# Last layer's attention: fp32 products of 8 rows become bf16 products of 24 rows in three passes

## The chip, the cores and the metric

The kernel runs on one core of a Trainium2 chip. The metric is the device time of one execution in microseconds. All durations below come from one profiled execution and its trace.

## The reference

The reference is a small network of four layers. Each layer normalises x, runs a token mixer s and a feed-forward g on the normalised x, and adds s times silu(g) to x. There are 4 batches of 1024 tokens with 128 channels. Only the last layer is touched here. Its mixer is causal attention with relative positions: 16 heads of 8 channels.

```python
qx, kx, vx = (split_head(x @ W.T) for W in (Wq, Wk, Wv))       # [b, 16, n, 8]
ex = rel_embed[ns].reshape(n, NH, HD).transpose(1, 0, 2)       # [16, n, 8]
srel = srel_skew(jnp.einsum('bhnd,hmd->bhnm', qx, ex))         # pad one column left, reshape, cut
qk = (jnp.einsum('bhnd,bhmd->bhnm', qx, kx) + srel) * inv_dim
atten = jax.nn.softmax(qk - mask, axis=-1)
out = jnp.einsum('bhnm,bhmd->bhnd', atten, vx).transpose(0, 2, 1, 3).reshape(b, n, d)
return out @ Wp.T + bp
```

Here n is 1024 and `ns` counts from -768 to 255, while the table `rel_embed` has 256 rows. The kernel therefore computes the relative term for a band near the diagonal from differences to the table's first row, and further keys get the plain product of q and k. Two einsums, q times k and q times the embeddings, contract over the 8 channels of a head; these two are what the change rewrites.

## The kernel before

Layers 0 to 2 run one after another over all batches and fill the first two thirds of the time. The last layer works batch by batch (`b`), in groups of four heads (`i` = 0 to 3, so 16 groups in all), and within a group over eight tiles of 128 queries (`t`, in the order 7, 0, 6, 1, 5, 2, 4, 3). A batch, group and tile together are a unit.

`prepare3` builds the weights once: transposes of Wq, Wk, Wv and Wp, and the embedding table `emb`. The four heads of a group sit on partitions 0, 32, 64 and 96, eight rows each, so that TensorE can work on four row groups side by side. POOL spreads the table into a zeroed `pad` (L1650), TensorE transposes it, and the first row is subtracted (L1657, L1658).

`begin3` prepares one batch: it loads x, normalises it (`layernorm`: batch-norm instructions on DVE, L136 and L137, square root and scaling on ACT, L138 and L143), transposes it, multiplies by Wq and Wk (L1832), copies the products on ACT (L1833) and stores q and k in DRAM (L1834). For batches 1 to 3 it is a generator that is advanced one step per unit beside the previous batch. `project3` loads q and k of one group back into SBUF, eight rows per head (L1882).

`relative3` multiplies two blocks of q with the table for two heads (L1911). ACT copies the product to a tile `r` (L1913), and SP stores it in a DRAM tile `flat` (L1916, L1917). `shear3` reads `flat` back on a slant into `rel` (L1932 to L1938) and POOL masks it (L1942). The loads for a unit are issued three units ahead.

`scores3` is the core. For each unit and each stretch of up to 512 keys it takes the single PSUM tile `sc`, does four score matmuls (L1975), one per head, and then compares on DVE, head by head: L1983 for keys beyond the band and L1990 for those with a relative term. Both scale, write `neg` and keep the running minimum `low`. After the last stretch ACT takes the exponential (L1997). There are 192 such score tiles. DVE then transposes the weights in blocks of 32 (L1734), one or two score tiles later, and `weigh3` multiplies them with the values (L2011). `finish3` and `end3` normalise, project and store.

`sc` has one buffer (four banks of PSUM), `tr` has three and `o` one. The pool `temp` has three buffers, shared by x, xn, the tiles of q, k and v in `begin3`, the tiles `h` and `up` of the feed-forward and all tiles `r`. The loop in `layer3` sets the rough order by advancing the generators; a compile-time scheduler then orders the instructions of each engine by its own estimates. Every engine, SP's DMA queue included, runs its instructions in that order.

Of the kernel before, what the change touches and what calls it, by code (L numbers as in the profile page):

```python
# [19 lines left out]
P = 128  # L20
NB = 4
T = 1024
# [1592 lines left out]

def spread(a):

    return a.rearrange("p (i j r) -> p i j r", j=4, r=32)[:, :, :, 0:8]


def heads_of(a):
    return a.rearrange("p (i j d) -> p i j d", j=4, d=8)


def prepare3(k, w, W, ps):
    nc = k.nc
    new = lambda name, shape: w.tile(shape, F32, tag=name, name=name)
    for name in ("Wq", "Wk", "Wv"):
        W[name + "T"] = new(name + "T", [P, D])
        k.transpose_tiles(ps, "tr", [W[name]], W[name + "T"])  # L1630

    W["WpB"] = new("WpB", [P, 4, 4, D])
    with k.tc.tile_pool(name="wide3", bufs=1) as rp:
        wide = rp.tile([P, 4, 4, 4, 8], F32, tag="wide", name="wide")
        for a in range(4):
            nc.gpsimd.tensor_copy(wide[:, :, :, a, :], W["Wp"].rearrange("p (i j d) -> p i j d", j=4, d=8))
        for i in range(4):
            pt = ps.tile([P, P], F32, tag="tr", name="pt")
            nc.tensor.transpose(pt, wide[:, i].rearrange("p j a d -> p (j a d)"), k.ident)
            for a in range(4):  # L1640
                nc.vector.tensor_scalar(W["WpB"][:, i, a, :], pt, k.c("of_a")[:, a : a + 1], None, op0=ALU.mult)
    W["bpw"] = new("bpw", [P, D])
    nc.gpsimd.tensor_copy(W["bpw"], W["bp"])
    W["emb"] = new("emb", [P, 4, 256])
    with k.tc.tile_pool(name="pad3", bufs=1) as rp:
        pad = rp.tile([P, 2, 512], F32, tag="pad", name="pad")
        nc.vector.memset(pad, 0.0)
        for c in range(2):
            for i in range(4):
                nc.gpsimd.tensor_copy(spread(pad[:, c, :])[:, i], heads_of(W["rel"][:, c, :])[:, i])  # L1650
        for i in range(4):
            k.transpose_tiles(ps, "tr", [pad[:, c, i * P : (i + 1) * P] for c in (0, 1)], W["emb"][:, i, :])

        e0 = rp.tile([P, 4], F32, tag="e0", name="e0")
        nc.vector.tensor_copy(e0, W["emb"][:, :, 0])
        for i in range(4):
            nc.vector.tensor_scalar(W["emb"][:, i, :], W["emb"][:, i, :], e0[:, i : i + 1], None, op0=ALU.subtract)  # L1657
        nc.vector.tensor_scalar(W["emb"][:, :, 0], e0, -1.0, None, op0=ALU.mult)  # L1658
        for name in ("gate", "up", "down"):
            f = rp.tile([P, 3, D], F32, tag="f" + name, name="f" + name)  # L1660
            nc.vector.tensor_scalar(f, W[name], 1.0 / 127.0, None, op0=ALU.mult)
            W[name + "T"] = new(name + "T", [P, 3, D])
            k.transpose_tiles(ps, "tr", [f[:, c, :] for c in range(3)], W[name + "T"].rearrange("p c d -> p (c d)"))
# [146 lines left out]
def begin3(k, W, p1, p2, temp, ps, dram, x3, b, eps5, seq):  # L1810

    nc = k.nc
    x = load_x3(nc, temp, x3, b)
    xn = temp.tile([P, 2 * 4, D], F32, tag="temp", name="xn")
    k.layernorm(p2, x.rearrange("p h a d -> p (h a) d"), xn, eps5)
    yield
    seq["xnT"] = xnT = p1.tile([P, T], F32, tag="xnT", name="xnT")
    for half in range(2):
        pt = ps.tile([P, 4, P], F32, tag="tr", name="pt")
        for a in range(4):  # L1820
            nc.tensor.transpose(pt[:, a, :], xn[:, 4 * half + a, :], k.ident)
        dst = xnT[:, half * 512 : (half + 1) * 512].rearrange("p (t a i) -> p a t i", t=4, a=4)
        nc.scalar.copy(dst, pt.rearrange("p a (t i) -> p a t i", i=32))
        yield

    seq["qk"] = dram.tile([2, P, T], F32, tag="qk", name="qk")
    for n, name in enumerate(("WqT", "WkT")):
        qk = temp.tile([P, T], F32, tag="temp", name="qk")
        for half in range(2):
            tok = slice(half * 512, (half + 1) * 512)  # L1830
            pp = ps.tile([P, 512], F32, tag="tr", name="pp")
            nc.tensor.matmul(pp, W[name], xnT[:, tok], start=True, stop=True)  # L1832
            nc.scalar.copy(qk[:, tok], pp)  # L1833
        nc.sync.dma_start(out=seq["qk"][n], in_=qk)  # L1834
        yield
    v = temp.tile([P, NT, D], F32, tag="temp", name="v")
    for half in range(2):
        pv = ps.tile([P, 4, D], F32, tag="tr", name="pv")
        for t in range(4):
            at = (4 * half + t) * P  # L1840
            nc.tensor.matmul(pv[:, t, :], xnT[:, at : at + P], W["WvT"], start=True, stop=True)
        nc.scalar.copy(v[:, 4 * half : 4 * half + 4], pv)
    seq["vd"] = vd = dram.tile([T, D], F32, tag="vd", name="vd")
    nc.sync.dma_start(out=vd.rearrange("(t p) d -> p t d", p=P), in_=v)
# [27 lines left out]

def project3(k, p2, seq, i, group):

    nc = k.nc
    q = p2.tile([P, 1 + T], F32, tag="q", name="q")
    kk = p2.tile([P, T], F32, tag="k", name="k")
    nc.gpsimd.memset(q[:, 0:1], 0.0)
    group.update({"q": q, "k": kk, "sums": p2.tile([P, 4, NT], F32, tag="sums", name="sums")})
    for n, dst in ((0, q[:, 1:]), (1, kk)):  # L1880
        for j in range(4):
            nc.sync.dma_start(out=dst[32 * j : 32 * j + 8], in_=seq["qk"][n, 32 * i + 8 * j : 32 * i + 8 * j + 8])  # L1882
        yield


def values3(k, p1, seq, vb, i):
# [12 lines left out]
def relative3(k, W, temp, ps, flat, q, i, pair, jp):  # L1899

    nc = k.nc
    r = temp.tile([P, 2, 2, 256], F32, tag="temp", name="r")
    js = (2 * jp, 2 * jp + 1)
    pr = [ps.tile([P, 2, 256], F32, tag="tr", name="pr") for _ in js]
    for m in range(2):
        for j, to in zip(js, pr):
            at, t = slice(32 * j, 32 * j + 8), 2 * pair + m  # L1910
            nc.tensor.matmul(to[:, m, :], q[at, t * P : (t + 1) * P], W["emb"][at, i, :], start=True, stop=True)  # L1911
    for n, to in enumerate(pr):
        nc.scalar.copy(r[:, n], to)  # L1913
    rows = flat.rearrange("m j p u -> p j m u")
    for m in range(2):
        nc.sync.dma_start(out=rows[:, 2 * jp : 2 * jp + 2, m, 0:256], in_=r[:, :, m])  # L1916
        nc.sync.dma_start(out=rows[:, 2 * jp : 2 * jp + 2, m, 256:384], in_=r[:, :, m, 0:P])  # L1917
# [37 lines left out]
def scores3(k, p1, p2, ps, group, rel, t):  # L1955
# [5 lines left out]
    nc = k.nc  # L1961
    q, kk = group["q"], group["k"]
    n = (t + 1) * P
    at = lambda j: slice(32 * j, 32 * j + 8)
    size = "b" if t > 3 else "s"
    S = [(p2 if t > 3 else p1).tile([P, T if t > 3 else 512], F32, tag=f"S{size}{j}", name="neg") for j in range(4)]
    group["S", t] = S
# [3 lines left out]
    for first in range(0, n, 512):  # L1971
        last = min(first + 512, n)
        sc = ps.tile([P, 4, 512], F32, tag="sc", name="score")
        for j in range(4):
            nc.tensor.matmul(  # L1975
                sc[:, j, 0 : last - first], q[at(j), 1 + t * P : 1 + n], kk[at(j), first:last], start=True, stop=True
            )
        yield "products"
        for j in range(4):

            neg, m = S[j], low[j]
            if first < plain:
                nc.vector.tensor_scalar(  # L1983
                    neg[:, 0:plain], sc[:, j, 0:plain], -INV3, None, op0=ALU.mult, op1=ALU.min, accum_out=m[:, 0:1]
                )
                least[j] = m[:, 0:1]
            begin = max(first, plain)
            slot = min(t, 4) - t + begin // P
            here = m[:, 1:2] if first == 0 else m[:, 2:3]
            nc.vector.tensor_tensor_reduce(  # L1990
                out=neg[:, begin:last], in0=sc[:, j, begin - first : last - first],
                in1=rel[:, j, slot : slot + (last - begin) // P, :].rearrange("p s c -> p (s c)"),
                scale=-INV3, scalar=least[j], op0=ALU.add, op1=ALU.min, accum_out=here,
            )
# [144 lines left out]
```

## Time and profile before

| What | Value |
|---|---|
| median of 3 runs | 3289.05 us (3281.75 to 3289.76) |
| profiled execution, its own time | 3290.69 us |
| its span, first to last instruction | 3288.7 us |
| PE matmul busy | 2325.6 us (71%) |
| PE weight load busy | 1329.6 us (40%) |
| DVE busy | 2357.9 us (72%) |
| ACT busy | 1487.6 us (45%) |
| POOL busy | 1203.9 us (37%) |
| mean granted TensorE clock | 0.732 of full |
| last layer's score matmuls L1975 | 1536 records, 292.7 us busy |
| last layer's table matmuls L1911 | 1024 records, 240.8 us busy |
| comparisons L1990 | 768 instructions |
| weights times values L2011 | 10240 records, 242.2 us busy |
| DMA through SP's queue | 296.03 MB |

A row with a line number stands for all instructions of that line. "Busy" is the time in which at least one of them runs. One fp32 matmul of the program shows as two matmul records and two weight loads. "Idle before, releaser" is the time that an engine stood still before those instructions, and the instruction that ended it. The pages' rows of digits cut the span into 40 slices and give the busy share of each in tenths; PEclk is the granted clock in tenths.

### The profile page before, as it was taken

The page shows a single profiled execution, that of the slowest core. Times are in us where ns is not written, and L with a number is a line of the kernel's source. Part 1 is how long each engine was busy: PE and PEld are TensorE (multiplying, and loading weights), DVE is VectorE, ACT ScalarE, POOL GpSimd, SP SyncE. Part 2 cuts the span into 40 slices and gives each one's busy share as a digit, 9 for nine tenths or more (in the row PEclk, how much of TensorE's full clock was granted, in tenths as well). Part 3 has the DMA queues.
Part 4 walks back from the last instruction along what each step waited for, and adds up shares of the span by engine and source line. Part 5 has one row for each costly group of instructions (what it writes and reads, how often), then busy time and mean ns, then how long its engine had stood idle before and what let it go on. Part 6 is the DMA issues. An engine that isn't in the chain of part 4 may idle for free. (4 is left out here: it accounts for less than half of the span.)

```text
span 3288.7 us, 50603 instructions
## 1 busy us (share of the span) xinstructions
PE 2325.6 (71%) x18321; PEld 1329.6 (40%) x18321; DVE 2357.9 (72%) x5534; ACT 1487.6 (45%) x3248; POOL 1203.9 (37%) x1104
## 2 busy tenths in 40 slices
PE   5787776777776767966243772557888888888885
PEld 2555555222332323641001322344544555545553
DVE  5555545978888876566899878436778778777786
ACT  3555453433333334345132551125665665655663
POOL 3344434144434343224586323342322322322322
PEclk9888888688778878976555665565767766756776
DMA  3000000100000001210422445337676767766772
GB/s 86 5 1 1 1 1 11 23 0 0 1 0 0 0 0 58 97 64 21 116 80 79 106 102 118 106 95 229 172 213 201 199 204 204 200 205 193 198 227 72
DMA packets 396446, 303.46 MB, mean 92 GB/s; under 512 B 96272, under 2 KB 380812, under 8 KB 390564
## 3 DMA queue, kind: packets, MB, share of 16 engines
q1 hardware_dynamic: 395044, 296.03, 32.0%
q10 hardware_dynamic: 1152, 4.19, 0.4%
q8 instruction: 144, 2.36, 0.3%
q14 instruction: 106, 0.87, 0.1%
HBM read 160.63 MB, written 138.94 MB: 91 GB/s over the span
## 5 line engine op out<-in xcount | busy, mean ns | idle before, releaser
L1997 ACT ACTIVATE neg<-neg,low 128x640 f32<-128x640 f32 (+7 forms) x512 | 390.0, 763 | 163.4 <-DVE low L1990 163.2
L1942 POOL TENSOR_SCALAR_AFFINE_SELECT rel<-rel 128x512 f32<-128x512 f32 x288 | 179.2, 634 | 584.5 <-DMA rel<-flat 420.5
L1734 DVE STREAM_TRANSPOSE wT<-neg 128x640 f32<-128x640 f32 (+7 forms) x512 | 362.4, 754 | 7.4 <-ACT neg L1997 6.3
L1975 PE MATMUL score<-k,q 8*128 8x512 f32 (+3 forms) x1536 | 292.7, 737 | 94.0 <-DVE low L1990 93.6
L1990 DVE CUSTOM_DVE_ANT_0 neg<-score,rel,low 128x128 f32<-128x128 f32 (+3 forms) x448 | 217.5, 517 | 158.7 <-PE score L1975 111.2
L1911 PE MATMUL pr<-emb,q 8*128 8x256 f32 x1024 | 240.8, 556 | 42.2 <-ACT r L1913 28.4
L2011 PE MATMUL po<-wT,vb 128*32 128x64 f32 (+1 forms) x10240 | 242.2, 258 | 35.2 <-issue 19.7
L2011 PEld LDWEIGHTS po<-wT,vb 128*32 128x32 f32 x10240 | 207.2, 140 | 144.7 <-issue 79.5
L1913 ACT COPY r<-pr 128x512 f32<-128x512 f32 x256 | 138.4, 581 | 143.5 <-PE pr L1911 94.3
L1911 PEld LDWEIGHTS pr<-emb,q 8*128 8x128 f32 x1024 | 150.4, 262 | 121.6 <-ACT r L1913 65.1
L1990 DVE CUSTOM_DVE_ANT_0 neg<-score,rel 128x512 f32<-128x512 f32 (+3 forms) x320 | 149.4, 521 | 26.5 <-PE score L1975 9.3
L1975 PEld LDWEIGHTS score<-k,q 8*128 8x128 f32 x1536 | 103.5, 249 | 156.6 <-DVE low L1990 126.9
L214 PE MATMUL pt<-ident,three 128*24 128x128 bf16 x64 | 9.3, 299 | 215.7 <-DVE three L211 211.3
L835 PE MATMUL pg<-xnT,w 128*128 128x512 f32 x256 | 148.2, 662 | 6.7 <-DVE h L839 3.1
L788 POOL TENSOR_TENSOR prod<-rest,kv 128x2048 f32<-128x2048 f32 x32 | 145.2, 4574 | 18.4 <-ACT rest L778 18.4
L837 PE MATMUL pu<-xin,w 128*128 128x512 f32 x256 | 141.2, 635 | 13.7 <-DVE h L839 7.7
L826 PE MATMUL po<-h,w 128*128 128x512 f32 x256 | 131.4, 635 | 26.9 <-DVE h L839 26.9
L838 ACT ACTIVATE h<-pg 128x512 f32<-128x512 f32 x128 | 75.9, 595 | 156.8 <-PE pg L835 153.3
L1983 DVE TENSOR_SCALAR_CACHE_REDUCE neg<-score 128x384 f32<-128x384 f32 (+2 forms) x192 | 79.9, 416 | 69.4 <-PE score L1975 69.4
L1452 PE MATMUL read<-kt,const_sb 128*128 128x128 f32 x256 | 51.3, 378 | 97.8 <-POOL kt L1447 97.8
L1050 PE MATMUL ph<-xin,upT 128*128 128x512 bf16 (+1 forms) x128 | 70.9, 586 | 64.7 <-DVE xin L1044 64.4
L431 PE MATMUL px<-hT,xbcT 128*128 128x512 f32 x256 | 115.8, 597 | 0.0
(621 smaller groups left out, 5788.7 us busy)
## 6 DMA issues: line engine op xcount, KB each, us to landing
flat<-r SPq DMA_DIRECT2D x256, 256.0 KB
rel<-flat SPq DMA_DIRECT2D x112, 512.0 KB
flat<-r SPq DMA_DIRECT2D x256, 128.0 KB
rel<-flat SPq DMA_DIRECT2D x96, 256.0 KB
kt<-kd SPq DMA_DIRECT2D x16, 512.0 KB
qt<-qd SPq DMA_DIRECT2D x16, 512.0 KB
kdc<-kdd SPq DMA_DIRECT2D x16, 512.0 KB
ktc<-ktd SPq DMA_DIRECT2D x16, 512.0 KB
```

The lines of the kernel that those rows point to most:

```text
L788: nc.gpsimd.tensor_tensor(prod, attn.rearrange("p (t h g) -> p t h g", t=4, g=16)[:, t].unsqueeze(2).to_broadcast(each), kv[:, t, 1, :].re ...
L826: nc.tensor.matmul(po, W["w2"][:, e, c, :], h[:, c, :], start=(e == 0 and c == 0), stop=(e == 7 and c == 1))
L835: nc.tensor.matmul(pg, W["w1"][:, e, c * P : (c + 1) * P], xnT, start=True, stop=True)
L837: nc.tensor.matmul(pu, W["w3"][:, e, c * P : (c + 1) * P], xin, start=True, stop=True)
L1734: nc.vector.transpose(weights[at, pair][j][:, t % 2, 0 : (t + 1) * P], S[j][:, 0 : (t + 1) * P])
L1911: nc.tensor.matmul(to[:, m, :], q[at, t * P : (t + 1) * P], W["emb"][at, i, :], start=True, stop=True)
L1913: nc.scalar.copy(r[:, n], to)
L1942: nc.gpsimd.affine_select(out=rel[:, :, slot(back), :], in_=rel[:, :, slot(0), :], compare_op=op, fill=fill, base=0, pattern=[[0, 4], [-si ...
L1975: nc.tensor.matmul(sc[:, j, 0 : last - first], q[at(j), 1 + t * P : 1 + n], kk[at(j), first:last], start=True, stop=True)
L1990: nc.vector.tensor_tensor_reduce(out=neg[:, begin:last], in0=sc[:, j, begin - first : last - first], in1=rel[:, j, slot : slot + (last - b ...
L1997: nc.scalar.activation(neg[:, 0:n], neg[:, 0:n], AF.Exp, bias=here, scale=-1.0, accum_out=group["sums"][:, j, t : t + 1])
L2011: nc.tensor.matmul(o[32 * j : 32 * j + 32, 2 * pair + m.start : 2 * pair + 2, :], vb[:, kb, j].rearrange("p a d -> p (a d)"), weights[j][: ...
```

## The change

q, k and the embeddings are each written as a sum of three bf16 numbers: the value rounded to bf16, the remainder rounded, and the remainder of that. On the contraction axis q has 24 rows per head, three thirds for each of 8 channels. The other operand holds one of its own thirds per pass, repeated three times over those rows, and three passes accumulate in PSUM, so that all nine products of thirds are summed.

- `prepare3` repeats each channel three times in the padded table and splits the transposed fp32 table into three bf16 tables with ACT copies and DVE subtractions.
- `begin3` splits each half of q and k with an ACT copy, a DVE subtraction, an ACT copy and a POOL subtraction, in two tiles of `temp` per half. It stores q once and k three times, and yields after each half.
- `project3` loads 24 rows per head: q of 2 bytes a token, k of three times 2 bytes.
- `relative3` and `scores3` make three bf16 matmuls per product instead of one fp32 matmul, with the thirds in the outer loop and the heads in the inner one.

```diff
 def spread(a):
-    return a.rearrange("p (i j r) -> p i j r", j=4, r=32)[:, :, :, 0:8]
+    return a.rearrange("p (i j r) -> p i j r", j=4, r=32)[:, :, :, 0:24].rearrange("p i j (d a) -> p i j d a", a=3)
...
-    W["emb"] = new("emb", [P, 4, 256])
+    W["emb"] = w.tile([P, 3, 4, 256], BF16, tag="emb", name="emb")
...
-                nc.gpsimd.tensor_copy(spread(pad[:, c, :])[:, i], heads_of(W["rel"][:, c, :])[:, i])
+                for a in range(3):
+                    nc.gpsimd.tensor_copy(spread(pad[:, c, :])[:, i, :, :, a], heads_of(W["rel"][:, c, :])[:, i])
+        emb = rp.tile([P, 4, 256], F32, tag="emb32", name="emb")
...
+        for third in range(3):
+            nc.scalar.copy(W["emb"][:, third], emb)
+            if third < 2:
+                nc.vector.tensor_tensor(emb, emb, W["emb"][:, third], ALU.subtract)
...
-    seq["qk"] = dram.tile([2, P, T], F32, tag="qk", name="qk")
-    for n, name in enumerate(("WqT", "WkT")):
-        qk = temp.tile([P, T], F32, tag="temp", name="qk")
+    seq["q"] = dram.tile([P, 3, T], BF16, tag="qd", name="qd")
+    seq["k"] = dram.tile([P, 3, 3, T], BF16, tag="kd", name="kd")
+    for name in ("WqT", "WkT"):
         for half in range(2):
             tok = slice(half * 512, (half + 1) * 512)
             pp = ps.tile([P, 512], F32, tag="tr", name="pp")
             nc.tensor.matmul(pp, W[name], xnT[:, tok], start=True, stop=True)
-            nc.scalar.copy(qk[:, tok], pp)
-        nc.sync.dma_start(out=seq["qk"][n], in_=qk)
-        yield
+            three = temp.tile([P, 3, 512], BF16, tag="temp", name="three")
+            rest = temp.tile([P, 512], F32, tag="temp", name="rest")
+            nc.scalar.copy(three[:, 0], pp)
+            nc.vector.tensor_tensor(rest, pp, three[:, 0], ALU.subtract)
+            nc.scalar.copy(three[:, 1], rest)
+            nc.gpsimd.tensor_tensor(three[:, 2], rest, three[:, 1], ALU.subtract)
+            if name == "WqT":
+                nc.sync.dma_start(out=seq["q"][:, :, tok], in_=three)
+            else:
+                for a in range(3):
+                    nc.sync.dma_start(out=seq["k"][:, a, :, tok], in_=three)
+            yield
...
-    q = p2.tile([P, 1 + T], F32, tag="q", name="q")
-    kk = p2.tile([P, T], F32, tag="k", name="k")
-    nc.gpsimd.memset(q[:, 0:1], 0.0)
+    q = p2.tile([P, 2 + T], BF16, tag="q", name="q")
+    kk = p2.tile([P, 3, T], BF16, tag="k", name="k")
+    nc.gpsimd.memset(q[:, 0:2], 0.0)
...
-            nc.sync.dma_start(out=dst[32 * j : 32 * j + 8], in_=seq["qk"][n, 32 * i + 8 * j : 32 * i + 8 * j + 8])
+        nc.sync.dma_start(out=q[32 * j : 32 * j + 24, 2:], in_=seq["q"][head].rearrange("d a t -> (d a) t"))
...
+        nc.sync.dma_start(out=kk[32 * j : 32 * j + 24], in_=seq["k"][head].rearrange("d a b t -> (d a) b t"))
...
-            at, t = slice(32 * j, 32 * j + 8), 2 * pair + m
-            nc.tensor.matmul(to[:, m, :], q[at, t * P : (t + 1) * P], W["emb"][at, i, :], start=True, stop=True)
+        first = 1 + (2 * pair + m) * P
+        for third in range(3):
+            for j, to in zip(js, pr):
+                at = slice(32 * j, 32 * j + 24)
+                nc.tensor.matmul(
+                    to[:, m, :], q[at, first : first + P], W["emb"][at, third, i, :], start=(third == 0), stop=(third == 2)
+                )
...
-        for j in range(4):
-            nc.tensor.matmul(
-                sc[:, j, 0 : last - first], q[at(j), 1 + t * P : 1 + n], kk[at(j), first:last], start=True, stop=True
-            )
+        for third in range(3):
+            for j in range(4):
+                nc.tensor.matmul(
+                    sc[:, j, 0 : last - first], q[at(j), 2 + t * P : 2 + n], kk[at(j), third, first:last],
+                    start=(third == 0), stop=(third == 2),
+                )
```

More of the change, by code (lines that the diff above doesn't have):

```diff
@@ L1649, in prepare3 @@
             for i in range(4):
-                nc.gpsimd.tensor_copy(spread(pad[:, c, :])[:, i], heads_of(W["rel"][:, c, :])[:, i])
+                for a in range(3):
+                    nc.gpsimd.tensor_copy(spread(pad[:, c, :])[:, i, :, :, a], heads_of(W["rel"][:, c, :])[:, i])
+        emb = rp.tile([P, 4, 256], F32, tag="emb32", name="emb")
         for i in range(4):
-            k.transpose_tiles(ps, "tr", [pad[:, c, i * P : (i + 1) * P] for c in (0, 1)], W["emb"][:, i, :])
+            k.transpose_tiles(ps, "tr", [pad[:, c, i * P : (i + 1) * P] for c in (0, 1)], emb[:, i, :])
         e0 = rp.tile([P, 4], F32, tag="e0", name="e0")
-        nc.vector.tensor_copy(e0, W["emb"][:, :, 0])
+        nc.vector.tensor_copy(e0, emb[:, :, 0])
         for i in range(4):
-            nc.vector.tensor_scalar(W["emb"][:, i, :], W["emb"][:, i, :], e0[:, i : i + 1], None, op0=ALU.subtract)
-        nc.vector.tensor_scalar(W["emb"][:, :, 0], e0, -1.0, None, op0=ALU.mult)
+            nc.vector.tensor_scalar(emb[:, i, :], emb[:, i, :], e0[:, i : i + 1], None, op0=ALU.subtract)
+        nc.vector.tensor_scalar(emb[:, :, 0], e0, -1.0, None, op0=ALU.mult)
+        for third in range(3):
+            nc.scalar.copy(W["emb"][:, third], emb)
+            if third < 2:
+                nc.vector.tensor_tensor(emb, emb, W["emb"][:, third], ALU.subtract)
         for name in ("gate", "up", "down"):
@@ L1875, in project3 @@
     nc = k.nc
-    q = p2.tile([P, 1 + T], F32, tag="q", name="q")
-    kk = p2.tile([P, T], F32, tag="k", name="k")
-    nc.gpsimd.memset(q[:, 0:1], 0.0)
+    q = p2.tile([P, 2 + T], BF16, tag="q", name="q")
+    kk = p2.tile([P, 3, T], BF16, tag="k", name="k")
+    nc.gpsimd.memset(q[:, 0:2], 0.0)
     group.update({"q": q, "k": kk, "sums": p2.tile([P, 4, NT], F32, tag="sums", name="sums")})
-    for n, dst in ((0, q[:, 1:]), (1, kk)):
-        for j in range(4):
-            nc.sync.dma_start(out=dst[32 * j : 32 * j + 8], in_=seq["qk"][n, 32 * i + 8 * j : 32 * i + 8 * j + 8])
-        yield
+    for j in range(4):
+        head = slice(32 * i + 8 * j, 32 * i + 8 * j + 8)
+        nc.sync.dma_start(out=q[32 * j : 32 * j + 24, 2:], in_=seq["q"][head].rearrange("d a t -> (d a) t"))
+    yield
+    for j in range(4):
+        head = slice(32 * i + 8 * j, 32 * i + 8 * j + 8)
+        nc.sync.dma_start(out=kk[32 * j : 32 * j + 24], in_=seq["k"][head].rearrange("d a b t -> (d a) b t"))
+    yield
 def values3(k, p1, seq, vb, i):
@@ L1908, in relative3 @@
     for m in range(2):
-        for j, to in zip(js, pr):
-            at, t = slice(32 * j, 32 * j + 8), 2 * pair + m
-            nc.tensor.matmul(to[:, m, :], q[at, t * P : (t + 1) * P], W["emb"][at, i, :], start=True, stop=True)
+        first = 1 + (2 * pair + m) * P
[5 more added lines that the diff above has]
+                )
     for n, to in enumerate(pr):
@@ L1963, in scores3 @@
     n = (t + 1) * P
-    at = lambda j: slice(32 * j, 32 * j + 8)
+    at = lambda j: slice(32 * j, 32 * j + 24)
     size = "b" if t > 3 else "s"
@@ L1973, in scores3 @@
         sc = ps.tile([P, 4, 512], F32, tag="sc", name="score")
-        for j in range(4):
-            nc.tensor.matmul(
-                sc[:, j, 0 : last - first], q[at(j), 1 + t * P : 1 + n], kk[at(j), first:last], start=True, stop=True
-            )
+        for third in range(3):
+            for j in range(4):
+                nc.tensor.matmul(
+                    sc[:, j, 0 : last - first], q[at(j), 2 + t * P : 2 + n], kk[at(j), third, first:last],
+                    start=(third == 0), stop=(third == 2),
+                )
         yield "products"
```

## The prediction

> **What bounds the kernel now.** I read four views: the page for the stages, the table by stretches of time for the last layer, the waits inside it, and the timeline for single tiles. Only the last layer is touched: it runs from about 2185 us to the end, its score stream from 2216.57 us (first L1975) to 3265 us.
>
> ```profile
> span 3288.7 us, 50603 instructions
> PE   5787776777776767966243772557888888888885
> DVE  5555545978888876566899878436778778777786
> PEclk9888888688778878976555665565767766756776
> ```
>
> The right half of each row is the last layer: neither PE nor DVE is full, and TensorE's granted clock is about two thirds. The stretches (span, PE, PE load, DVE, ACT, POOL busy, clock, DMA share, GB/s) say the same:
>
> ```profile
> 1900.00:2000.00 100.00, 65.04 (x203) 28.72 (x202) 74.91 (x194) 51.80 (x108) 22.80 (x16) 0.67 0.49 108
> 2200.00:2400.00 200.00, 160.53 (x1985) 104.15 (x1987) 126.66 (x407) 116.04 (x260) 51.19 (x75) 0.65 0.72 206
> 2600.00:2800.00 200.00, 169.22 (x2810) 104.84 (x2809) 159.04 (x507) 119.67 (x284) 51.98 (x73) 0.67 0.71 208
> ```
>
> Two engines at 75 to 85% suggest alternation. The waits of that window (engine, line, releaser: us, times, longest) show it:
>
> ```profile
> POOL rel L1942 <- DMA rel<-flat: 420.5, 80, 16.0
> PEld score L1975 <- DVE low L1990: 126.9, 99, 11.0
> DVE neg L1990 <- PE score L1975: 120.5, 63, 6.8
> DVE neg L1983 <- PE score L1975: 69.4, 15, 25.2
> ```
>
> There is one score tile in PSUM: PE waits until DVE has compared all four heads, then DVE waits for the next scores. Going through the 192 score tiles record by record, in 102 the first comparison starts within 0.22 us of the last score matmul; DVE is idle 228 us there. Score matmuls fill 188 us of those intervals, and in 77 us PE is still busy with something else (weights times values 23, feed-forward 27, table products L1911 11). In the other 90 tiles DVE is still transposing, and a shorter score gives nothing. POOL's 420 us on loads is no bound: DVE waits for POOL's result 17.7 us in all.
>
> **The change: cheaper matmuls.** The granted clock has two values, 0.5 and 1. The timeline has both for the eight records of one tile (start, duration):
>
> ```profile
> 2639.66 1.18 PE L1975 MATMUL score<-k,q 8*128 8x512 f32 x8
> 2645.36 2.07 PE L1911 MATMUL pr<-emb,q 8*128 8x256 f32 x8 [0.92 <-ACT r L1913]
> 2651.36 1.24 PE L1975 MATMUL score<-k,q 8*128 8x256 f32 x8 [0.66 <-DVE low L1990]
> 2654.73 2.09 PE L1975 MATMUL score<-k,q 8*128 8x512 f32 x8 [0.94 <-DVE low L1990]
> ```
>
> At half clock 256 more columns cost 0.85 us, 3.32 ns each: four passes of 0.83 ns. Each fp32 product is two records of two passes, the four heads side by side. At full clock (1.14 for 512, 0.71 for 256) it is 1.7 ns. For bf16 at 24 rows the trace has a near row, the routing product of the expert layers:
>
> ```profile
> L222 PEld LDWEIGHTS <-pick x128: 90/98/110, 623.9 to 1947.8; 24*128 24x128 bf16 x128
> L222 PE MATMUL pb<-thirds,pick x128: 371/580/629, 623.9 to 1947.8; 24*128 24x512 bf16 x128
> ```
>
> One bf16 pass of 512 columns, alone, is 0.60 us at half and 0.37 at full clock. Three are 0.60+2x0.425=1.45 against 2.09, and 0.37+2x0.225=0.82 against 1.14. For 256 columns: 0.82 against 1.24, and 0.48 against 0.71. The table product of two heads (12 records instead of 8) goes from about 2.07 to 1.6 at half clock, 1.13 to 0.85 at full. Clipping each score saving by DVE's idle time, with the clock each tile had, leaves 37 us of the 102 tiles.
>
> The built program's order changes too: the scheduler weighs the new matmuls by its own costs. So I summed all 192 steps: a step is the comparison of four heads, then the later of (transposes behind it) and (next score plus whatever PE work between the two scores overruns the comparison). Prices are the rows above; weights times values 46 matmuls in 2.58 us cold and 1.53 warm; 64% of the time at half clock (0.68 mean). Old order and prices: 1098 us against 1045 measured, 5% too much. Old order, new prices: 1032, so **-66**. New order, new prices: 1084, **-14**. The order gives 52 back: in groups 4, 8 and 12, 158 weights-times-values matmuls (45 ns each, 7.1 us) and some 38 table matmuls (4 us) stand between the two score tiles of t=5, where there were 82 and 1. Comparing takes 3.5 us there, so the next score is some 7 us late; what moved up had been hidden later on. I take -14, with -45 (the order costs a third) and +10 as ends.
>
> **The clock.** The last layer's PE is 82 to 86% busy at 0.65 to 0.73; the stretch 1900 to 2000 is 65% busy and has 0.67, so by these rows the clock does not follow the load, and nothing is added. The Trainium skill ("TensorE: Matmul & The Clock Gate", "What's actually happening") speaks against the change: half speed is the default and some 3.4 us of activity releases it, so PE work cut by a sixth may spend more time cold. With 72% instead of 64% at half clock the sum is 1103, 20 us more. Nearer to the row, I take +4; end +20.
>
> **Start of the layer.** Nothing covers it. The padding is filled by 24 POOL copies instead of 8, 0.204 us each (L1650): +3.3. Then three ACT copies (1.14 us for 128x1024, L1997) and two DVE subtractions (about 1.2 from 0.69 for 128x512, L1582) alternate, and in the new order the batch-norm aggregate of the first batch is behind the second subtraction, ACT's square root behind the third copy. The last table instruction ended at 2190.67, now 2194.0, plus 5.7 gives 2199.7 for the square root:
>
> ```profile
> 2193.55 0.30 ACT L138 ACTIVATE ln_rs<-ln_mv,eps 128x8 f32<-128x8 f32 x1 [3.42 <-DVE ln_mv L137]
> 2200.14 0.58 ACT L1833 COPY qk<-pp 128x512 f32<-128x512 f32 x1 [1.48 <-PE pp L1832]
> 2202.11 2.06 SPq L1834 DMA_DIRECT2D qk<-qk  x2
> 2208.44 0.58 ACT L1913 COPY r<-pr 128x512 f32<-128x512 f32 x1 [2.85 <-PE pr L1911]
> ```
>
> So +6.1. Then each half of q or k is ACT 0.58, DVE 0.69, ACT 0.58, POOL 1.2 (half of 2.34 for 128x1024, L228), DMA 2.4 (from issue at 2202.11 to the reload): 5.4 us. Each takes two of the three buffers of `temp`, so the second remainder waits for the first half's store to land, and so on; four halves come one after another, and the first `r` waits for the last k store. Without the shift of 6.1 that is 2220.9 instead of 2208.44, +12.5. The table products are ready by then and the copies run closer together: -2.6. Together **+16** (+8 if the chain overlaps better, +22 if reloads collide).
>
> **Three batch switches.** The same split runs between score tiles: four DVE subtractions (4x0.69=2.8 us), four more ACT copies (2.3), four POOL subtractions behind selects that wait for loads, eight stores instead of two on SP, each waiting for POOL with the table stores and `rel` loads queued behind. Each subtraction waits for ACT's copy, which stands behind four exponentials (up to 4.6 us), and for a `temp` buffer whose table stores must land; the next comparison is behind it. No row shows this wait. Lower bound -2 us a switch, since a scheduler can place it where DVE idles and the old switch already costs (groups with one last about 69 us by the starts of their first comparisons, plain ones 58); upper bound four waits of 2.5. Nearest to the old one I take 3.3 each, **+10** (-6 to +30).
>
> **Traffic.** q and k go out as 3.15 MB a batch instead of 1.05, and come back the same: 16.8 MB more than 296. DMA is 0.71 busy; loads are issued ahead and DVE rarely waits, so 0; without that cover +10. The loads of q and k stay at eight DMAs a group, q's wider memset is 0.1 us, hidden.
>
> **Sum.** -14+4+16+10=+16. The profiled execution took 3290.69 (span 3288.7, 2.0 around it), 1.6 above the median: 3307 there, **3305** for the median.
>
> **Rivals.** Faster: cheap products win. For: 190 us of DVE waits end at the score, and a saving of 66 at the old order. Against: the new order and the start. If its loss is a third, -45+16+5=-24, 3265; it decides once the steps save over 26. 25%.
> No change: the four terms cancel within 10 us (0.3%, about what a measurement tells here). 15%.
> Much slower: the bf16 weight loads of four row groups don't run side by side as the fp32 ones do. Then a pass costs 4x0.098=0.39 us of loads, at full clock more than the 0.22 of streaming: 0.5 us a tile on a third of the tiles, +32; or subtractions block DVE at the switches, +30. 3335. 13%.
> That bf16 is not used where claimed I exclude: the built program has bf16 loads there.
> The likeliest, 3300 to 3330: 47%. So faster 0.25, same 0.15, slower 0.60. The range, 3257 to 3352, takes the faster case whole and the doubled costs.
>
> **What would show it.** Right: score tiles of 512 columns at 1.45 and 0.82 us; first `r` copy some 16 us later after the last store of layer 2; DVE waiting for ACT or DMA at the subtraction; longer PE clusters before the second tile of t=5. Wrong: DVE's waits for scores falling from 190 to under 140 without other waits growing; a clock well off 0.68; score tiles no shorter.

## The result and the profile after

The changed kernel takes 3308.57 us (median of 4 runs, 3303.89 to 3310.52) against 3289.41 (3281.75 to 3290.05) for the kernel before on the same chip: a ratio of 1.0062, 95% interval 1.0043 to 1.0080. It is slower by 0.6%, with 3305 forecast. The profiled spans are 3308.8 and 3288.7 us.

The page of the changed kernel (busy share in tenths of 40 slices, and the granted clock):

```profile
PE   5787786777776767956233662546777777777775
DVE  5555455978878876666999878436788687688676
PEclk9898888688778878976555665566766867766776
```

In the right half PE has come down from eights to sevens; DVE and the clock have hardly moved. One stretch of the changed kernel (start:end, length, PE, PE load, DVE, ACT, POOL busy, clock, DMA share, GB/s):

```profile
2600.00:2800.00 200.00, 150.91 (x2930) 93.09 (x2929) 158.55 (x506) 123.67 (x296) 59.63 (x81) 0.70 0.77 222
```

TensorE works 18 us less than before in these 200 us, and VectorE gets no more done. The DMA share went from 0.71 to 0.77. The matmuls became as short as forecast. From the timeline of the changed kernel (start, duration), the tiles of 512 and 256 columns, each at half and at full clock:

```profile
2694.94 1.47 PE L2001 MATMUL score<-k,q 24*128 24x512 bf16 x12
2715.79 0.83 PE L2001 MATMUL score<-k,q 24*128 24x512 bf16 x12 [0.64 <-DVE low L2017]
...
2667.06 0.83 PE L2001 MATMUL score<-k,q 24*128 24x256 bf16 x12 [2.43 <-DVE low L2017]
2677.40 0.51 PE L2001 MATMUL score<-k,q 24*128 24x256 bf16 x12
```

The waits of the changed kernel from 2185 us to the end (engine, line, releaser: us, times, longest):

```profile
DVE neg L2017 <- issue: 90.7, 30, 11.3
DVE neg L2017 <- POOL rel L1967: 53.8, 11, 17.1
DVE neg L2017 <- PE score L2001: 45.1, 23, 9.3
DVE neg L2010 <- PE score L2001: 17.7, 1, 17.7
```

Read quickly, VectorE's wait for scores has dropped from 190 to 63 us, and other waits have taken its place ("issue" is idle time for which the view shows no releaser). That reading is too good. A comparison waits for several things, and the view names the one that it saw last. The timeline of group 4 in the changed kernel shows one "issue" wait as what it is:

```profile
2533.33 3.75 PE L2038 MATMUL po<-wT,vb 128*32 128x64 f32 x164
...
2537.78 1.35 PE L2038 MATMUL po<-wT,vb 128*32 128x64 f32 x90
...
2540.35 0.93 PE L2038 MATMUL po<-wT,vb 128*32 128x64 f32 x62 [1.22 <-issue]
...
2541.21 1.07 PE L1934 MATMUL pr<-emb,q 24*128 24x256 bf16 x18
...
2543.17 1.02 PE L2001 MATMUL score<-k,q 24*128 24x256 bf16 x6
...
2544.32 0.48 DVE L2017 CUSTOM_DVE_ANT_0 neg<-score,rel,low 128x256 f32<-128x256 f32 x1 [4.78 <-issue]
```

The score tile ends at 2544.19 and the comparison starts 0.13 us later. VectorE waited 4.78 us for TensorE, which stood still for 1.2 us, multiplied weights with values and q with the table, and only then came to the tile. So I went through the records of all 192 score tiles. Where the first comparison starts within 0.3 us of the tile's last matmul, VectorE's idle time ahead of it is a wait for the score: "executing" while the tile runs, "PE late" before it begins. All other idle time in the stream is "rest". (A wait that ends together with the tile may have had a second cause that ended earlier; the records don't show it.) The columns add up to the stream, from the first comparison to the last (us):

| kernel | first comparison | stream | VectorE busy | executing | PE late | rest |
|---|---|---|---|---|---|---|
| before | 2219.5 | 1045.1 | 805.5 | 139.7 | 57.6 | 42.3 |
| changed | 2234.4 | 1050.0 | 803.1 | 75.8 | 94.7 | 76.4 |
| e1 old order, bf16 | 2239.9 | 1066.9 | 813.9 | 93.4 | 92.9 | 66.8 |
| e5 own order, bf16 | 2239.3 | 1070.9 | 803.5 | 76.0 | 118.4 | 73.0 |
| e8 half relative scores, bf16 | 2235.0 | 980.2 | 799.5 | 65.5 | 58.3 | 56.9 |
| e9 half relative scores, fp32 | 2221.7 | 1021.6 | 804.4 | 121.2 | 50.4 | 45.6 |
| e10 one third of the keys, bf16 | 2230.3 | 1011.4 | 799.2 | 64.1 | 79.8 | 68.4 |
| e11 wide loads, fp32 | 2221.7 | 1041.3 | 804.8 | 139.8 | 54.2 | 42.5 |

The 20.1 us between the spans are 14.9 at the start (0.4 of it from before the last layer), 4.9 in the stream and 0.3 after it. Within the stream the shorter matmuls did bring 64 us under executing tiles. Against that stand 37 more because PE reached the tile late and 34 more in the rest. VectorE's own work, some 800 us, is the floor.

Both can be taken apart further in the same records. Of the 37 us of "PE late", 35 arise at one place, ahead of the second score tile of t=5: 0.4 before and 17.9 after in groups 4, 8 and 12, and 15.7 before and 33.4 after in groups 1, 5, 9 and 13, where the feed-forward stands in front of that tile. In the rest, VectorE's transposes of the weights wait 7 us before and 24 after (for ScalarE and TensorE), comparisons wait 17 and 27 (mostly for relative scores), and the new subtraction 6.5.

By groups of four heads (time between first comparisons of successive groups, summed, us):

| kernel | groups 4, 8, 12 | groups 3, 7, 11 (next batch prepared) | the other ten |
|---|---|---|---|
| before | 179.8 | 208.2 | 657.1 |
| changed | 201.4 | 195.4 | 653.2 |
| e1 old order, bf16 | 189.3 | 232.5 | 645.1 |
| e5 own order, bf16 | 219.1 | 199.8 | 652.0 |
| e2 new order, fp32 | 224.0 | 194.8 | 700.6 |
| e12 own order, fp32 | 205.3 | 225.4 | 691.4 |
| e10 one third of the keys, bf16 | 181.9 | 187.2 | 642.3 |

### The profile page after: what moved, and what is told of

Its sections match the earlier page's. It is cut to its first block, busy times and chain, and to the rows that moved or that the text cites. A ratio compares the mean times of both kernels' runs of the same rounds, so it can differ in the third digit from the quotient of the medians.

```text
span 3308.8 us, 53103 instructions
## 1 busy us (share of the span) xinstructions
PE 2209.7 (67%) x19601; PEld 1257.4 (38%) x19601; DVE 2359.5 (71%) x5552; ACT 1498.2 (45%) x3267; POOL 1225.3 (37%) x1136
## 3 DMA queue, kind: packets, MB, share of 16 engines
q1 hardware_dynamic: 409252, 312.82, 33.6%
## 5 line engine op out<-in xcount | busy, mean ns | idle before, releaser
L2001 PE MATMUL score<-k,q 24*128 24x512 bf16 (+3 forms) x2304 | 205.2, 436 | 157.8 <-DVE low L2017 151.3
L2038 PE MATMUL po<-wT,vb 128*32 128x64 f32 (+1 forms) x10240 | 235.0, 249 | 68.4 <-issue 43.4
L2038 PEld LDWEIGHTS po<-wT,vb 128*32 128x32 f32 x10240 | 197.4, 133 | 148.7 <-issue 84.6
L1934 PE MATMUL pr<-emb,q 24*128 24x256 bf16 x1536 | 190.9, 355 | 54.1 <-ACT r L1938 27.2
L1934 PEld LDWEIGHTS <-q 24*128 24x128 bf16 x1536 | 112.2, 117 | 128.8 <-issue 83.3
L2001 PEld LDWEIGHTS <-q 24*128 24x128 bf16 x2304 | 71.5, 108 | 230.5 <-issue 188.3
L783 DVE TENSOR_REDUCE s<-prod 128x128 f32<-128x2048 f32 x32 | 73.1, 2284 | 49.6 <-POOL prod L788 49.6
```

The costliest lines, as they stand in the source:

```text
L1934: nc.tensor.matmul(to[:, m, :], q[at, first : first + P], W["emb"][at, third, i, :], start=(third == 0), stop=(third == 2))
L2001: nc.tensor.matmul(sc[:, j, 0 : last - first], q[at(j), 2 + t * P : 2 + n], kk[at(j), third, first:last], start=(third == 0), stop=(third ...
L2038: nc.tensor.matmul(o[32 * j : 32 * j + 32, 2 * pair + m.start : 2 * pair + 2, :], vb[:, kb, j].rearrange("p a d -> p (a d)"), weights[j][: ...
```

## The experiments

Times are medians, ratios are to the kernel before on the same chip.

**Order.** In e1 and e2 the instruction order of one kernel is written out in the other, as edges of issue order between successive instructions. `ORDER` holds one list of instructions per engine (cut here), for the loop of the last layer: TensorE, VectorE, GpSimd and ScalarE without its copies of the table product. SP's queue is left to the scheduler in bf16; in fp32 its stores and loads of relative scores are listed too.

```diff
         while weighs:
             step()
+        pin(k)
+
+
+def pin(k):
+
+    made = {i.name: i for i in k.nc.cur_bb.bb.instructions}
+    order = mybir.DependencyInfo(mybir.DependencyClass.NoSync, mybir.DependencyReason.DATA)
+    for steps in ORDER.values():
+        n, before = 0, None
+        for step in steps.split():
+            n += int(step)
+            if before is not None:
+                k.tc.add_manual_dep(made[f"I-{n}"], before, order, reason="pinned order")
+            before = f"I-{n}"
...
```

> The changed kernel with the instruction order of the kernel before written out for the loop of the last layer on TensorE, VectorE, GpSimd and ScalarE (except the copies of the table product): the three-pass bf16 matmuls stand exactly where the fp32 ones stood. Nothing is left out. Theory A, the prediction's first step (at the old order the cheaper matmuls are worth about 66 us, and the new order gives about 52 of it back): the start stays late by about 15 us (first compare at about 2234), the stream of scores from the first compare to the end falls from 1050 to about 990 to 1000 us, the time to about 3250 to 3260; groups 4, 8 and 12 fall from 65 to 70 us each to under 61. Rival B, the order matters only for the clusters seen in groups 4, 8 and 12, and elsewhere VectorE and the loads of the relative scores bound already: the stream loses 20 to 25 us, time 3283 to 3289. Rival C, the order is of no account and what the shorter matmuls freed has gone to other waits: 3303 to 3313.

Measured: 3330.96 us, ratio 1.0129 (1.0114 to 1.0144): none of the three theories, slower than the changed kernel.

> The other corner: the kernel before with its fp32 matmuls, and the loop of the last layer in the instruction order of the changed kernel on TensorE, VectorE, GpSimd, ScalarE (except the copies of the table product) and for the loads and stores of the relative scores. Nothing is left out. Theory A: the new order by itself costs about 50 us of the stream, so 3289 goes to about 3335 to 3345, the first compare staying at 2219 to 2221. Rival B: the clusters of groups 4, 8 and 12 alone, 3309 to 3315. Rival C: the order is of no account, 3284 to 3294.

Measured: 3370.45 us, ratio 1.0260 (1.0241 to 1.0279), more than any theory said. Two orders that both lose point at the method, so I ran each kernel with its own order written out in the same way.

> Control of the method of the four runs before: the changed kernel with its own order written out in the same way (loop of the last layer, TensorE, VectorE, GpSimd, ScalarE without the copies of the table product; the queue of loads and stores on SP is left to the scheduler, as there). Nothing is left out. If writing an order out is neutral: 3303 to 3314, the groups as in the changed kernel within 2 us each, and the 22 us by which the old order was slower and the 74 us by which the single key store was slower are theirs. If the method itself shifts the queue on SP: above 3320, and only what the earlier runs have above this one is theirs.

Measured: 3335.57 us, ratio 1.0140 (1.0102 to 1.0179). The method costs 27 us by itself (why is open).

> Control for the fp32 kernel in the changed kernel's order (3370): the kernel before with its own order written out by the same method, queue of relative scores included. Nothing is left out. If the method costs the fp32 kernel what it costs the bf16 one (27 us): 3310 to 3320, and the changed kernel's order costs the fp32 matmuls 50 to 60 us. If the method is neutral here: 3285 to 3295, and the order's price is some 80 us. If it is 3350 or more, the order's price is 20 us or less.

Measured: 3369.93 us, ratio 1.0234 (1.0210 to 1.0259); in fp32 the method costs 80 us.

Only pairs made in the same way can be compared. bf16: old order 3331.0, new order 3335.6. fp32: new order 3370.5, own order 3369.9. In both pairs the order of the listed engines as a whole comes out even, with intervals of 0.15 to 0.4% either way on each ratio; a difference of some 13 us would go unseen, one of 52 would not. In the bf16 pair SP's queue may differ too. By groups the orders do differ: in bf16 the new order costs 29.8 us in groups 4, 8 and 12 (219.1 against 189.3) and saves 32.8 in groups 3, 7 and 11. In fp32 it is 18.7 and 30.7. One comparison shows the cost in groups 4, 8 and 12: the one after the second score tile of t=5 in group 4. First e1, with the old order, then e5, with the new one (timelines of VectorE):

```profile
2567.02 0.48 DVE L2270 CUSTOM_DVE_ANT_0 neg<-score,rel,low 128x256 f32<-128x256 f32 x1 [1.19 <-POOL rel L2220]
```

```profile
2559.83 0.48 DVE L2272 CUSTOM_DVE_ANT_0 neg<-score,rel,low 128x256 f32<-128x256 f32 x1 [10.46 <-POOL rel L2222]
```

The wait is 1.19 us with the old order and 10.46 with the new one. The label is wrong here too: in e5 the tile's last score matmuls run from 2558.67 to 2559.69. In the 10.46 us PE also stood still for 3.5.

The feed-forward's part of "PE late" does not go with the order. Ahead of the second tile of t=5 in groups 1, 5, 9 and 13 it is 32.9 us in e1, 33.0 in e5, 30.3 in e2 and 31.6 in e12, against 15.7 before. What doubled it is open.

**Stores and loads of the keys.** e3 keeps the changed kernel's order (written out, so e5 is its reference) and stores the thirds of k once; e4 does the same with the old order.

```diff
...
-                for a in range(3):
-                    nc.sync.dma_start(out=seq["k"][:, a, :, tok], in_=three)
+                nc.sync.dma_start(out=seq["k"][:, :, tok], in_=three)
...
-        nc.sync.dma_start(out=kk[32 * j : 32 * j + 24], in_=seq["k"][head].rearrange("d a b t -> (d a) b t"))
+        for a in range(3):
+            nc.sync.dma_start(out=kk[32 * j + a : 32 * j + 24 : 3], in_=seq["k"][head])
```

> The changed kernel, its order of the loop kept, with the three thirds of the keys written once to DRAM (two stores a batch in place of six, and a third of the bytes) and read three times, by 12 loads of 8 rows a group in place of 4 of 24. Nothing is left out. Theory (the start is late by the q and k chain, and part of that is the queue of six key stores in front of the q loads): the first compare comes 3 to 6 us earlier than 2234, the time falls to 3302 to 3306. Rival, the split chain and the layer norm alone set the start and the q loads would have come no earlier: first compare at 2234 within 1 us, time 3308 within 3. Rival, the 8 more loads a group on SP delay the rel loads behind them: waits of VectorE for the rel loads grow over the 54 us of the changed kernel, time 3312 or more.

Measured: 3382.64 us, ratio 1.0286 (1.0271 to 1.0302), 47 us above e5. The first comparison is at 2239.2 and 2239.3, so the start gained nothing. SP's queue in e3, at the loads of the keys of group 5:

```profile
2563.15 7.75 SPq L2158 DMA_DIRECT2D k<-kd  x12
2570.99 0.39 SPq L2212 DMA_DIRECT2D rel<-flat  x1
```

In e5 the loads of the same group:

```profile
2531.07 0.47 SPq L2158 DMA_DIRECT2D k<-kd  x1
...
2546.04 1.28 SPq L2158 DMA_DIRECT2D k<-kd  x3
```

Twelve issues in one block take 7.75 us where four took 1.75, and the load of a relative-score tile stands behind them. The kernel moves 6.3 MB less (306.53 against 312.82) and loses 2.9 us a group. Of the 47 us, 30 arise at the feed-forward (63.2 us of "PE late" ahead of the second tile of t=5 in groups 1, 5, 9 and 13, against 33.0 in e5). That the longer issues did it is likely, but not shown alone: the loads also write every third partition, and the scheduler ordered SP's queue anew.

> Both together: keys stored once and read three times, and the order of the kernel before in the loop of the last layer with the bf16 matmuls. Nothing is left out. Theory A with the start as expected: 3245 to 3256, the best of the four. Rival B: 3278 to 3286. Rival C: 3300 to 3310.

Measured: 3403.56 us, ratio 1.0346 (1.0330 to 1.0361): the two don't help each other.

**Is it SP's queue?** e6 and e7 move the 12 loads of q, k and v of a group to ScalarE's queue, e6 in the changed kernel, e7 in the one before; the scheduler orders both anew.

```diff
-        nc.sync.dma_start(out=q[32 * j : 32 * j + 24, 2:], in_=seq["q"][head].rearrange("d a t -> (d a) t"))
+        nc.scalar.dma_start(out=q[32 * j : 32 * j + 24, 2:], in_=seq["q"][head].rearrange("d a t -> (d a) t"))
...
```

> The changed kernel with the loads of q, k and v of each group (12 issues a group, about 0.45 to 1.0 us each, some 7 us of SP's time a group) issued by ScalarE in place of SP; order left to the scheduler; nothing left out. Theory D (after the change the step loop hangs on the tiles of relative scores, and what holds those is SP's queue, in which their stores and loads stand behind other issues and waits): 3 to 6 us less a group, 3210 to 3260, and VectorE's waits for rel (issue, POOL rel, rel loads, together some 155 us in the loop) fall by half. Theory E (the transfers themselves hold them, not the queue): 3300 to 3312. Rival F (ScalarE's exponentials become late by its new issues, 6 us a group): 3320 or more.

Measured: 3319.44 us, ratio 1.0097 (1.0058 to 1.0135), 11 us above the changed kernel; the two intervals overlap.

> The same edit on the kernel before (fp32 matmuls, 12 issues a group moved from SP to ScalarE); nothing left out. If the fp32 kernel hung mainly on its score tiles (163 us of VectorE's waits in the loop against 37 for rel): 3270 to 3290, less than half of what the changed kernel gains. If both kernels hang on SP's queue alike: the same gain as the changed kernel, so 3190 to 3240 if that one reaches 3210 to 3260.

Measured: 3309.63 us, ratio 1.0051 (1.0034 to 1.0068).

Taking these 12 loads off SP's queue gains nothing, so theory D falls as far as it rests on them. The order of the stores and loads that stay in the queue is another matter (see below). Where the loads went they were in the way: in e6 ScalarE's copies of the table product waited 14.0 us for `k<-kd` and 33.6 us for stores of `flat` to land, in the changed kernel 5.4 and 4.6 us. The Trainium skill ("DMA: Bandwidth & Descriptors", "Issuing engines are not separate DMA queues") says why little was to be had: DMAs started by different engines run on the same 16 DMA engines, and only the time to start them is saved. No run here separates the two.

**Is it the bytes?** e8 keeps the relative scores in bf16 on their way through DRAM in the changed kernel, e9 in the kernel before.

```diff
-                    flats[at, pair] = dram.tile([2, 4, P, 384], F32, tag="flat", name="flat")
+                    flats[at, pair] = dram.tile([2, 4, P, 384], BF16, tag="flat", name="flat")
...
-    r = temp.tile([P, 2, 2, 256], F32, tag="temp", name="r")
+    r = temp.tile([P, 2, 2, 256], BF16, tag="temp", name="r")
...
-    rel = pool.tile([P, 4, min(t, 4) + 1, P], F32, tag="relb" if t > 3 else f"rels", name="rel")
+    rel = pool.tile([P, 4, min(t, 4) + 1, P], BF16, tag="relb" if t > 3 else f"rels", name="rel")
```

> The changed kernel with the relative scores stored and loaded in bf16 (r, the flat table in DRAM and the rel tiles): half the bytes of the 352 us worth of stores and loads, the same number of issues; precision is left out. Theory E (the transfers hold the loop): 3220 to 3280, and GpSimd's waits for rel loads, 332 us between 2400 and 3250, fall by a third or more. Theory D (the queue, not the bytes): 3298 to 3312. If neither bounds, 3303 to 3313 with the waits moved.

Measured: 3245.57 us, ratio 0.9868 (0.9832 to 0.9905), 63 us under the changed kernel. It beats both kernels, for less precise relative scores. The instructions on them did not become shorter (GpSimd's mask 636 ns against 637, ScalarE's copy 580 against 581), so that is not the cause.

> The kernel before (fp32 matmuls) with the relative scores stored and loaded in bf16, as in the run of the changed kernel that took 3246; precision is left out. It completes a square: matmuls fp32 or bf16, relative scores fp32 or bf16. Theory E' (before the change the loop hangs mainly on the score tiles of TensorE, after it on the transfers of the relative scores): halving them gives the fp32 kernel much less than the 63 us it gave the changed one, 3265 to 3285, so that with half the bytes the change is worth 20 to 40 us. Rival G (the transfers bound both alike): 3220 to 3232, and the change costs about 20 us with half the bytes too.

Measured: 3265.20 us, ratio 0.9914 (0.9891 to 0.9937). Halving is worth 25 us to the fp32 kernel and 63 to the bf16 one. With half the bytes the change gains 20 us by the medians, 15 by the ratios (the two intervals just overlap), with all of them it loses 19. In e8 the DMA queue has as many packets as in the changed kernel (409252) and moves 220.54 MB in place of 312.82.

e10 goes at the change's own traffic: only the first third of each key is stored and loaded, and used in all three passes.

```diff
...
-                    nc.sync.dma_start(out=seq["k"][:, a, :, tok], in_=three)
+                    nc.sync.dma_start(out=seq["k"][:, a, tok], in_=three[:, 0])
...
-        nc.sync.dma_start(out=kk[32 * j : 32 * j + 24], in_=seq["k"][head].rearrange("d a b t -> (d a) b t"))
+        nc.sync.dma_start(out=kk[32 * j : 32 * j + 24, 0], in_=seq["k"][head].rearrange("d a t -> (d a) t"))
...
-                    sc[:, j, 0 : last - first], q[at(j), 2 + t * P : 2 + n], kk[at(j), third, first:last],
+                    sc[:, j, 0 : last - first], q[at(j), 2 + t * P : 2 + n], kk[at(j), 0, first:last],
```

> The changed kernel with only the first third of each key stored and loaded (an eighth of the bytes less in all that q and k move: 12.6 MB less), and this third used in all three passes; the number of matmuls, stores and loads is the same. The remainders of the keys are left out of the computation. If the 16.8 MB that the change adds are what eats the shorter matmuls: 3265 to 3290. If traffic of this size costs nothing, as the prediction had it: 3300 to 3310, with at most 1 to 3 us at the start from smaller stores.

Measured: 3264.32 us, ratio 0.9911 (0.9888 to 0.9935): 44 us under the changed kernel with 12.6 MB less (300.23 MB). (The expectation calls that an eighth of what q and k move; 12.6 of their 25.2 MB is half.)

e11 adds traffic to the kernel before: its loads of q and k take 24 rows where 8 are used.

> The kernel before with its loads of q and k made three times as wide (24 rows where 8 are used, for all but the last heads), about 8 MB more, the increase of loads that the change brings; every engine's instruction order is that of the kernel before, nothing is left out. If traffic costs time in the fp32 kernel: 3300 to 3320. If it is hidden there: 3285 to 3293. With the run of the single key third it says whether the prediction's zero for the traffic holds in one kernel, in both or in neither.

```diff
-            nc.sync.dma_start(out=dst[32 * j : 32 * j + 8], in_=seq["qk"][n, 32 * i + 8 * j : 32 * i + 8 * j + 8])
+            at = 32 * i + 8 * j
+            rows = min(24, P - at)
+            nc.sync.dma_start(out=dst[32 * j : 32 * j + rows], in_=seq["qk"][n, at : at + rows])
```

Measured: 3294.72 us, ratio 1.0010 (0.9998 to 1.0022), with 7.6 MB more (303.64 MB). In the fp32 kernel, whose row in the table of waits hardly moves either, such loads are as good as hidden.

e10 needs a caution. With smaller loads the scheduler ordered the kernel otherwise, and the cluster ahead of the second tile of t=5 was gone (82 weights-times-values matmuls instead of 158); the same holds for e8. So part of the 44 us is order: groups 4, 8 and 12 make up 19.5. In groups 0, 1, 2, 14 and 15 PE's order is nearly that of the changed kernel, and there e10 takes 9.0 us less and e8 15.0. But SP's queue is ordered otherwise there too. Group 1 alone has 5.7 of e10's 9.0, and most of it can be read at one place. The timeline of the changed kernel, in group 1, with SP's queue:

```profile
2295.57 0.51 SPq L1941 DMA_DIRECT2D flat<-r  x1
2304.49 0.38 SPq L1959 DMA_DIRECT2D rel<-flat  x1
2304.92 0.50 SPq L1942 DMA_DIRECT2D flat<-r  x1
...
2310.55 0.92 ACT L1879 COPY up<-pgu 128x256 f32<-128x256 f32 x3 [3.25 <-DMA flat<-r]
...
2311.79 3.62 PE L1884 MATMUL po<-downT,h 128*128 128x128 f32 x12 [2.21 <-POOL h L1880]
...
2316.76 1.15 PE L2001 MATMUL score<-k,q 24*128 24x512 bf16 x12
...
2317.97 0.75 DVE L2017 CUSTOM_DVE_ANT_0 neg<-score,rel,low 128x512 f32<-128x512 f32 x1 [5.69 <-PE score L2001]
```

The same place in e10:

```profile
2289.01 1.12 SPq L1941 DMA_DIRECT2D flat<-r  x1
...
2291.27 0.51 SPq L1942 DMA_DIRECT2D flat<-r  x1
...
2300.45 0.38 SPq L1959 DMA_DIRECT2D rel<-flat  x1
...
2308.79 0.75 DVE L2017 CUSTOM_DVE_ANT_0 neg<-score,rel,low 128x512 f32<-128x512 f32 x1 [0.94 <-PE score L2001]
```

`up` comes from `temp`, whose three buffers also hold the table products `r`. ScalarE can't fill it until a store of `r` has landed, 3.25 us; POOL then forms `h` late, PE waits for `h` piece by piece, and the score tile stands behind that in PE's order. The store was not slow, it was issued late. In the changed kernel a load of `rel` (L1959) stands in SP's queue between the first store of this `r` and its other three, and it waited for VectorE:

```profile
SPq L1959 <- DVE low L2017: 8.3, 1, 8.3
```

The three stores went out from 2304.92 on. In e10 all four had gone out by 2291.8, ahead of that load. So this wait comes from the order of SP's queue and not from the bytes, and no view of VectorE's waits names it. It is also the only time in the last layer of the changed kernel that `up` waits for a store. The other four groups of equal PE order leave 3.3 us to e10, with SP's order different there as well. So e10 shows what fewer bytes and the order that came with them are worth together, 44 us. The same holds for e8 and e9. Bytes alone, in the bf16 kernel and at an unchanged order, were not tried.

## Why the prediction was right or wrong

The time was right, and so were several terms. Two large terms, -66 for the cheaper matmuls and +52 for the order, were wrong and cancelled. So the sum of the stream was right by luck.

- **Score tiles and table products.** Right. Tiles of 512 columns took 1.47 and 0.83 us (forecast 1.45 and 0.82), of 256 columns 0.83 and 0.51 (0.82 and 0.48). The bf16 weight loads of four row groups do run side by side, so that rival is out.
- **Start, +16.** Right in sum: +14.9 at the first comparison. The square root came 4.8 us later (6.1 forecast), the first `r` copy 18.2 later (18.6 by the working, 6.1 and 12.5; its list of signs says 16), and the ready table products then made up 3.3 of it (2.6). In the working the four halves take 4 times 5.4 us from 2200.14, which is 2221.7 and not 2220.9. The two ends in the timeline of the changed kernel:

```profile
2198.39 0.30 ACT L138 ACTIVATE ln_rs<-ln_mv,eps 128x8 f32<-128x8 f32 x1
...
2225.03 1.82 PE L1934 MATMUL pr<-emb,q 24*128 24x256 bf16 x15 [10.82 <-DMA q<-qd]
2226.68 1.07 ACT L1938 COPY r<-pr 128x512 f32<-128x512 f32 x2 [6.92 <-PE pr L1934]
```

- **Clock, +4.** Nothing happened: 0.733 against 0.732 for the whole, 0.70 against 0.67 in the stretch from 2600, where PE's busy share fell from 85% to 75%. The clock was at half for 63% of the stream before and 61% after; 64 and 72% had been reckoned with. The Trainium skill ("TensorE: Matmul & The Clock Gate", "What's actually happening") says that the slow clock is the default and that activity lifts it; the 20 us that the prediction worked out in case it spends more time cold did not come, and the row was the better guide. What share of activity holds the clock is not shown here.
- **"Old order, new prices: 1032, so -66" and "the order gives 52 back".** Gain and loss are both there in the trace (64 us under executing tiles; 37 and 34 back), but the loss was put down to the wrong thing. The clusters of groups 4, 8 and 12 are real: +21.6 us in the changed kernel, and 30 or 19 between the orders of one kernel. But the same new order saves as much where the next batch is prepared. In sum the order is worth nothing that these runs could see in either kernel (e1 against e5, e2 against e12). For the old order the working gave a stream of 1032 us. e1's stream is 1066.9, of which some 21 are the method's (e5's 1070.9 against 1050.0), so about 1046. That is an estimate, for the method need not cost the old order what it costs the new one. By it the whole change at the old order brings the stream nothing against 1045.1, where 66 had been reckoned. The step that failed is this -66. The step sum counted PE's work between two scores at fixed prices, and nothing else that could hold PE or VectorE. It had no term for PE itself waiting there (6.8 us of "PE late" before, 20.9 after), for the feed-forward's part growing (17.7 us more ahead of t=5), or for VectorE's other waits in the rest (34 us more).
- **Batch switches, +10.** Wrong in sign: groups 3, 7 and 11 take 12.8 us less. The split itself hardly held anything up (ACT copy ahead of the subtraction: 12.1 us in three waits in all). In both pairs the new order is some 31 to 33 us shorter there. At equal order the bf16 kernel takes 5 to 7 us more there than the fp32 one, its shorter matmuls included (e5 against e2, e1 against e12, whose lists are not quite alike). So the split may well cost what was forecast, and the order hides it. (Two slips of the working: the plain groups took 58 to 64 us before, not 58; and the sum of the rival "faster" puts 5 for clock and switches where the forecast has 14.)
- **Traffic, 0.** Open. It holds in the fp32 kernel, where 7.6 MB more of loads cost 4.8 us (ratio interval from -0.02% to +0.22%). In the changed kernel 12.6 MB less went with 44 us, more than the +10 given for lost cover, but the order changed with the bytes: 19.5 lie in groups 4, 8 and 12, where the clusters went, and 5.7 in group 1, most of it from the order of SP's queue. What the bytes alone cost is not shown.
- **"Wrong if" the waits for scores fall without others growing.** They fell from 190 to 63 by the view, to 171 from 197 by the records; others did grow.

Not all of the 71 us that stand against the gain has a cause. By place, 35 are PE late ahead of the second tile of t=5. The half of them in groups 4, 8 and 12 goes with the order, which gives as much back at the switches. The half at the feed-forward is open, and so is what delays VectorE in the rest.

## What to carry to other kernels

A cheaper matmul is worth only what the rest of the loop leaves of it: here the same change loses 19 us, and with the relative scores at half their bytes it gains 15 to 20. An edit that changes bytes can change the compile-time order too, of the DMA queue as well; compare the order of every queue before the gain is put down to the bytes. A new compile-time order moves losses between stages; judge it over the whole loop, and against a control made by the same method. Before believing a table of waits, take a few of its entries in the timeline and look for what ended just before the wait did.

## What was not expected of the hardware

- Issues on SP take time of their own: four loads of 24 rows took 1.75 us of the queue in group 5, twelve of 8 rows 7.75 (e5, e3).
- One load at the head of SP's queue that waited 8.3 us for VectorE held back three ready stores behind it, and in the end a score tile.
- Three accumulating bf16 passes of 24 rows run back to back (0.83 us for 512 columns, four heads side by side, at full clock, where 0.82 was reckoned for one pass and twice its columns), with their 12 weight loads hidden.
- TensorE's granted clock, 0.67 to 0.73 in the five stretches from 2245 to 3200 us before, was 0.69 to 0.72 there after, though PE's busy time in them fell from 814.5 to 695.4 us.
